# An involution's columns: how many tiles go by products of 64 channels and how many by products of 32

## The chip, the cores and the metric

The kernel runs on one core of one Trainium2 chip. The metric is the device time of one execution in microseconds, as the median of several runs.

## The reference

Four layers follow one another on an input `x` of 4 images with 256 channels of 56 x 56, in 32-bit floats. Each normalizes its input in 32 groups (`_gn`), applies a block, and adds the block's result to its input. Layers 0 and 2 are involutions, and the change is in them. An involution is a 7 x 7 filter whose taps are computed for each position and for each of 16 groups of 16 channels:

```python
t = jnp.einsum('bchw,oc->bohw', x, w1)               # 256 -> 64
t = jax.nn.relu(_bn_eval(t, ...))                    # layer 2 only
wgt = jnp.einsum('bchw,oc->bohw', t, w2) + b2[None, :, None, None]
wgt = wgt.reshape(b, G, K * K, h, w)                 # 16 groups x 49 taps
patches = jnp.stack([xp[:, :, i:i + h, j:j + w] for i in range(K) for j in range(K)], axis=2)
patches = patches.reshape(b, G, GC, K * K, h, w)
out = jnp.einsum('bgkhw,bgckhw->bgchw', wgt, patches).reshape(b, c, h, w)
out = jax.nn.relu(_bn_eval(out, ...))                # layer 2 only
```

Layer 1 is two 3 x 3 convolutions with batch norms, layer 3 a gate from channel means and Fourier transforms. They are not touched.

## The kernel before

A unit of work is one image `b` and one half `cb` of its channels (128 channels on the 128 partitions); a layer has eight units, taken one after the other. In a unit the image is cut into tiles of 3 rows by 8 columns of pixels (`TY`, `TX`): 19 tiles, one below the other, make a column, and seven columns (`NTX`) make the image. The 19th tile has two rows of image and one row of padding.

A tile with its border of 3 is a window of 9 x 14 = 126 pixels (`Q`). `begin_windows` transposes a strip of the normalized image (`strip_sb`, one column with its border) on TensorE, line L406, in seven products of 128 x 126; ScalarE copies the result into `xw` (L418), and DMAs move its rows about to make the windows of all 19 tiles (L424 and L426; in layer 0 one of the four is issued by POOL, the others by SP; in layer 2 all by SP). There are three `xw` buffers. The strip is written by POOL in layer 0 (L391) and, after the first two strips, by ScalarE in layer 2 (L389). There is one strip buffer.

Ahead of a unit's columns, `tap_matrices` builds `kt`, which holds for each group, each pixel of a tile and each tile the 126 weights that this pixel applies to the window, by products on TensorE (L593), with evictions shared by VectorE (L611) and ScalarE (L604).

`apply` then does a column. For a tile it multiplies the windows by `kt` (L635). One product takes `ng * 16` channels and the weights of `ng` groups for 24 pixels, so that for each channel one of the `ng` results is the wanted one and the others are waste: with `ng` = 4 a tile takes two products of 64 channels by 96 columns, with `ng` = 2 it takes four of 32 channels by 48. `O_PARTS` says which tiles go which way:

```python
for ng, tys, nty, rows in O_PARTS:
```

Each entry has `ng`, the first tile of each PSUM bank used, the tiles in a bank, and the rows of pixels. The wanted results are then picked out by an accumulation over `ng` terms with a scale for each channel that is one or zero (in layer 2 it holds the batch norm's scale as well): the first term by ScalarE (L648 in layer 0, L650 in layer 2), each further one by VectorE (L655), into the tile `un`. At last `un` is added to the image: by POOL in layer 0 (L660), with a relu by VectorE in layer 2 (L662).

The order in a column is: the products and evictions of both parts (`apply`), the transposes and window copies for the column three further on (`next_windows`), the next strip (`next_strip`), and then smaller work of other stages that is put between columns: statistics of the column before (L1105), in layer 0 statistics of the next image (L359), in every second unit the 1 x 1 products of the next image's bottleneck (L469), in layer 2 loads and POOL arithmetic of the gate of the image before (L803 to L816). [...] PSUM is used through four slots of two banks each, taken in turn; a column takes three: one for each part and one for the transposes.

Of the kernel before, what the change touches and what calls it, by code (L numbers as in the profile page):

```python
# [10 lines left out]
F32 = mybir.dt.float32  # L11
# [5 lines left out]
P = 128  # L17
B, C, H, W = 4, 256, 56, 56
# [15 lines left out]
TY, TX = 3, 8  # L34
# [12 lines left out]

O_PARTS = ((4, (0, 5), 5, 30), (2, (10,), 9, 26))  # L50
NXW = 3


# [18 lines left out]
def net_kernel(  # L72
# [226 lines left out]
    def involution_layer(layer, xin, xout, red, span, sb, xs_of, ahead=None, pending=None):  # L299

        with ExitStack() as es:
            wpool = es.enter_context(tc.tile_pool(name="iw", bufs=1))
            big = es.enter_context(tc.tile_pool(name="ibig", bufs=1))
            work = es.enter_context(tc.tile_pool(name="iwork", bufs=2))
            banks = es.enter_context(tc.tile_pool(name="banks", bufs=4, space=PSUM))

            def two_banks():

                return banks.tile([P, 2, 512], F32, name="ps")
# [83 lines left out]
            def window(ty):  # L393

                k, j = divmod(ty, TY)
                return (0, NSB, 2 * NSB - 1)[j] + k
# [226 lines left out]
            def apply(b, cb, kt, tx, xw):  # L623

                img = xs_of[b, cb].rearrange("p (h w) -> p h w", w=W)
                y0 = 0
                for ng, tys, nty, rows in O_PARTS:
                    pair = two_banks()
                    nb, m = len(tys), ng * GC
                    v = pair[:, :nb, : ng * nty * TP].rearrange("p i (e n) -> p i e n", e=ng)  # L630
                    for i in range(nb):
                        for k in range(nty):
                            ty = tys[i] + k
                            for j in range(P // m):
                                nc.tensor.matmul(  # L635
                                    v[m * j : m * j + m, i, :, k * TP : (k + 1) * TP],
                                    xw[:, window(ty), m * j : m * j + m],
                                    kt[:, ng * j : ng * j + ng, :, ty * NTX + tx, :],
                                    start=True,
                                    stop=True,  # L640
                                )
                    n = rows // nb * TX
                    o = [v[:, :, e, :n] for e in range(ng)]
                    un = work.tile([P, 2, O_PARTS[0][3] // 2 * TX], F32, name="un")
                    un = un.rearrange("p i n -> p (i n)")[:, : rows * TX]
                    part = un.rearrange("p (i n) -> p i n", i=nb)
                    if layer == 0:
                        nc.scalar.mul(part, o[0], bn["par"][ng][:, 0:1])  # L648
                    else:
                        nc.scalar.activation(  # L650
                            part, o[0], AF.Identity, bias=bn["t4"][:, cb : cb + 1], scale=bn["s4"][ng][:, 0, cb : cb + 1]
                        )
                    for e in range(1, ng):
                        s = bn["par"][ng][:, e : e + 1] if layer == 0 else bn["s4"][ng][:, e, cb : cb + 1]
                        nc.vector.scalar_tensor_tensor(part, o[e], s, part, ALU.mult, ALU.add)  # L655
                    dst = img[:, y0 : y0 + rows, tx * TX : (tx + 1) * TX]
                    y0 += rows
                    u = un.rearrange("p (r x) -> p r x", x=TX)
                    if layer == 0:
                        nc.gpsimd.tensor_tensor(dst, u, dst, ALU.add)  # L660
                    else:
                        nc.vector.scalar_tensor_tensor(dst, u, 0.0, dst, ALU.max, ALU.add)  # L662
# [355 lines left out]
            for u, (b, cb) in enumerate(units):  # L1018
# [24 lines left out]
                if b + 1 < B:  # L1043
                    n = 16 if layer == 0 else (26, 21)[cb]
# [57 lines left out]
                img = xs_of[b, cb].rearrange("p (h w) -> p h w", w=W)  # L1102
# [4 lines left out]
                for tx in range(NTX):  # L1107
                    if layer == 2 and u == len(units) - 1 and tx == NTX - 1:
                        column_sums(tx - 1)
                    for f in early[tx]:  # L1110
                        f()
                    apply(b, cb, kt, tx, xws[u * NTX + tx])
                    next_windows()
                    next_strip()
                    if tx > 0 and not (layer == 2 and u == len(units) - 1 and tx == NTX - 1):
                        column_sums(tx - 1)
                    for f in late[tx]:
                        f()
# [640 lines left out]
```

## Time and profile before

| What | Value |
|---|---|
| Median of three runs | 1791.4 us (1791.14 to 1792.2) |
| The profiled execution, its span | 1791.4 us |
| TensorE products busy | 1716.7 us, 96% |
| TensorE weight loads busy | 1507.5 us, 84% |
| VectorE busy | 1385.3 us, 77% |
| ScalarE busy | 813.5 us, 45% |
| POOL busy | 406.2 us, 23% |
| Products of L635, recorded | 12544, 381.8 us busy |
| Columns of layer 0 | from 72 to 515 us |
| Convolutions of layer 1 | from 515 to 1250 us |
| Columns of layer 2 | from 1285 to 1758 us |

The page gives TensorE two rows: PE for products and PEld for weight loads, which overlap. Each product of the program stands in the records as two pairs of a weight load and a product. A group's busy time is the union of its spans, so that overlapping products count once, while the mean of one is its own length, most of which lies beside its neighbours. The timeline merges neighbouring instructions of one kind into one line with their number; a note in brackets gives the engine's idle time and what ended it, and "issue" stands for time in which the engine waited for nothing that is recorded. The SP rows of the timeline are the issues of DMAs, not the transfers.

### The profile page before, as it was taken

Reading aid. Unit: us, or ns where it says so; the run is one execution under the profiler, and the core shown is the slowest. Engines: PE = TensorE matmul, PEld = TensorE weight load, DVE = VectorE, ACT = ScalarE, POOL = GpSimd, SP = SyncE. Lnnn points to the kernel's source line nnn. Section 1 sums busy time; section 2 is a strip of 40 time slices with the busy share of each in tenths; the row PEclk is TensorE's granted clock in tenths of the full one; section 3 lists DMA queues with packets and bytes.
Section 4 is the critical chain, followed back from the end, with each engine's and each line's share of the span. In section 5 each row is a group of like instructions: output and inputs, shape, how many; then the busy total and the mean of one; then the engine's idle time right before and its main releaser. Section 6 shows DMA issues by size and latency. Waiting matters only on the chain.

```text
span 1791.4 us, 55774 instructions
## 1 busy us (share of the span) xinstructions
PE 1716.7 (96%) x24040; PEld 1507.5 (84%) x24040; DVE 1385.3 (77%) x2745; ACT 813.5 (45%) x1882; POOL 406.2 (23%) x627
## 2 busy tenths in 40 slices
PE   6999999999999999999999999999999999999998
PEld 4998988889978988898889888986888887788886
DVE  2777787767778988988898889885777778687775
ACT  2555556555533222222323132111767667567564
POOL 2224422444320000000000000001000355463572
PEclk9999999999989999999999999999999999999997
DMA  2445444633653021211111111122344567566653
GB/s 86 135 151 170 140 146 134 196 107 119 204 171 105 32 75 51 76 33 64 58 68 44 52 63 37 44 110 73 122 164 156 162 213 220 169 223 189 183 154 115
DMA packets 66003, 215.76 MB, mean 120 GB/s; under 512 B 13237, under 2 KB 20926, under 8 KB 62046
## 3 DMA queue, kind: packets, MB, share of 16 engines
q1 hardware_dynamic: 49262, 145.37, 25.9%
q0 software_dynamic: 14656, 64.77, 11.3%
q8 instruction: 190, 3.11, 0.7%
q10 hardware_dynamic: 1840, 2.05, 0.4%
q14 instruction: 55, 0.45, 0.1%
HBM read 76.30 MB, written 49.15 MB: 70 GB/s over the span
## 4 chain that ended last, share of the span: by engine, by line
PE 68%; DVE 19%; ACT 4%; DMA 4%; issue 3%; POOL 2%; SPq 1%; POOLq 0%; ACTq 0%; DVEq 0%
PE mm L1523 17%; PE ps L593 14%; PE ps L635 14%; PE mm L1441 9%; DVE kt L611 6%; PE mm L1412 5%; PE ps L406 3%; DMA xw<-xw 3%; DVE un L655 3%; PE ps L469 1%; DVE res L1516 1%; DVE xs L1375 1%; DVE st L1105 1%; ACT kt L604 1%; ACT hp L488 1%
## 5 line engine op out<-in xcount | busy, mean ns | idle before, releaser
L635 PE MATMUL ps<-kt,xw 126*32 126x48 f32 (+1 forms) x12544 | 381.8, 235 | 27.8 <-issue 12.2
L635 PEld LDWEIGHTS ps<-kt,xw 126*32 126x32 f32 (+1 forms) x12544 | 341.9, 121 | 74.5 <-issue 45.5
L593 PE MATMUL ps<-hp,z_sb 64*126 64x133 f32 x6144 | 383.2, 279 | 8.4 <-DVE kt L611 4.6
L1523 PE MATMUL mm<-v,u_sb 128*128 128x280 f32 (+1 forms) x1728 | 383.5, 383 | 1.9 <-DVE u_sb L1254 1.5
L593 PEld LDWEIGHTS ps<-hp,z_sb 64*126 64x126 f32 x6144 | 363.6, 185 | 24.4 <-DVE kt L611 6.8
L611 DVE TENSOR_TENSOR kt<-ps,zb_sb 126x798 f32<-126x798 f32 x352 | 332.9, 980 | 60.4 <-PE ps L593 49.2
L1523 PEld LDWEIGHTS mm<-v,u_sb 128*128 128x128 f32 x1728 | 326.1, 189 | 56.3 <-DVE u_sb L1254 1.9
L604 ACT ACTIVATE kt<-ps,zb_sb 126x133 f32<-126x133 f32 x960 | 280.1, 441 | 107.3 <-PE ps L593 107.3
L1441 PE MATMUL mm<-v,u_sb 128*128 128x252 f32 (+1 forms) x936 | 209.5, 384 | 0.0
L1441 PEld LDWEIGHTS mm<-v,u_sb 128*128 128x128 f32 x936 | 176.4, 189 | 30.5 <-issue 0.8
L655 DVE SCALAR_TENSOR_TENSOR un<-ps,s,un 128x240 f32<-128x240 f32 x224 | 102.6, 458 | 86.7 <-ACT un L650 79.9
L1560 POOL DMA_DIRECT2D x<-xs x24 | 13.1, 547 | 680.1 <-DVE xs L1559 426.5
L655 DVE SCALAR_TENSOR_TENSOR un<-ps,par_sb,un 128x240 f32<-128x240 f32 x224 | 98.1, 457 | 86.8 <-ACT un L648 82.3
L1508 ACT ACTIVATE res<-xs,shift,norm_sb 128x1120 f32<-128x1120 f32 (+1 forms) x24 | 30.2, 1258 | 236.3 <-DVE xs L1559 107.3
L418 ACT COPY xw<-ps 126x896 f32<-126x896 f32 x112 | 101.2, 905 | 44.0 <-PE ps L406 38.5
L406 PE MATMUL ps<-ident_sb,strip_sb 128*126 128x128 f32 x784 | 111.9, 283 | 8.4 <-POOL strip_sb L391 5.3
L660 POOL TENSOR_TENSOR xs<-un,xs 128x240 f32<-128x240 f32 x112 | 72.1, 664 | 192.2 <-DVE un L655 192.1
L648 ACT ACTIVATE un<-ps,par_sb 128x240 f32<-128x240 f32 x112 | 50.1, 448 | 122.5 <-PE ps L635 120.6
L650 ACT ACTIVATE un<-ps,bn_t,s 128x240 f32<-128x240 f32 x112 | 60.1, 537 | 94.7 <-PE ps L635 88.7
L406 PEld LDWEIGHTS ps<-ident_sb,strip_sb 128*126 128x126 f32 x784 | 85.1, 142 | 19.5 <-POOL strip_sb L391 8.3
L1412 PE MATMUL mm<-xs,u_sb 128*128 128x126 f32 (+1 forms) x792 | 98.7, 277 | 2.3 <-DVE xs L1375 1.3
L1412 PEld LDWEIGHTS mm<-xs,u_sb 128*128 128x128 f32 x792 | 94.4, 191 | 3.7 <-DVE xs L1428 1.6
(256 smaller groups left out, 1903.1 us busy)
## 6 DMA issues: line engine op xcount, KB each, us to landing
xw<-xw SPq DMA_DIRECT2D x168, 252.0 KB
xw<-xw SPq DMA_DIRECT2D x224, 126.0 KB
xw<-xw POOLq DMA_DIRECT2D x56, 252.0 KB, 4.6
xs<-x SPq DMA_DIRECT2D x24, 560.0 KB
x<-xs POOLq DMA_DIRECT2D x8, 1568.0 KB, 7.5
xs<-x SPq DMA_DIRECT2D x8, 1568.0 KB
xs<-in_x_dram SPq DMA_DIRECT2D x6, 1568.0 KB
x<-xs SPq DMA_DIRECT2D x6, 1568.0 KB
```

The costliest lines, as they stand in the source:

```text
L406: nc.tensor.transpose(ps[:Q, k * P : (k + 1) * P], flat[:, k * Q : (k + 1) * Q], ident_sb)
L418: nc.scalar.copy(xw[:, :NSB, :], ps[:Q, : NSB * P].rearrange("q (n c) -> q n c", n=NSB))
L593: nc.tensor.matmul(ps[:Q, i, k * NT : (k + 1) * NT], z_sb[i * R : (i + 1) * R, cb * GB // 2 + gp, z0 : z0 + Q], hp[i * R : (i + 1) * R, py ...
L604: nc.scalar.activation(kt[:, g0 + i, pb, :, k], ps[:Q, i, k * NT : (k + 1) * NT], AF.Identity, bias=zb_sb[:, cb * GB + g0 + i, p0 + k : p0 ...
L611: nc.vector.tensor_tensor(kt[:, g0 : g0 + 2, pb], ps[:Q, :, : PB * NT].rearrange("q i (k t) -> q i t k", k=PB), zb_sb[:, cb * GB + g0 : cb ...
L635: nc.tensor.matmul(v[m * j : m * j + m, i, :, k * TP : (k + 1) * TP], xw[:, window(ty), m * j : m * j + m], kt[:, ng * j : ng * j + ng, :, ...
L650: nc.scalar.activation(part, o[0], AF.Identity, bias=bn["t4"][:, cb : cb + 1], scale=bn["s4"][ng][:, 0, cb : cb + 1])
L655: nc.vector.scalar_tensor_tensor(part, o[e], s, part, ALU.mult, ALU.add)
L660: nc.gpsimd.tensor_tensor(dst, u, dst, ALU.add)
L1412: nc.tensor.matmul(ps[:, co * m : (co + 1) * m], u[ci][:, co * P : (co + 1) * P], v2[:, e, : n // 2, ci * WT : (ci + 1) * WT], start=(ci = ...
L1441: nc.tensor.matmul(ps, u1_sb[:, ci, dy, k, co * P : (co + 1) * P], v[:, k, dy * NB + ci : (dy + n - 1) * NB + ci + 1 : NB, :], start=(j == 0),
L1523: nc.tensor.matmul(ps, u2_sb[:, ci, dy, k, co * P : (co + 1) * P], v[:, k, dy * NB + ci : (dy + n - 1) * NB + ci + 1 : NB, :], start=(j == 0),
```

## The change

Ten tiles of a column went by products of 64 channels and nine by products of 32. Now the first three go by 64 and the other sixteen by 32. A column's products in the program are 6 and 64 where they were 20 and 36. The first part fills one bank with three tiles, where it filled two with five each; the second fills two banks with eight tiles each, where it filled one with nine. It now holds 48 rows of which 47 exist, so the addition to the image is cut to the rows that exist. The tile `un` becomes two tiles of one buffer each, one for each part and of its own size, where it was one tile of two buffers.

```diff
-O_PARTS = ((4, (0, 5), 5, 30), (2, (10,), 9, 26))
+O_PARTS = ((4, (0,), 3, 9), (2, (3, 11), 8, 48))
...
-                    un = work.tile([P, 2, O_PARTS[0][3] // 2 * TX], F32, name="un")
-                    un = un.rearrange("p i n -> p (i n)")[:, : rows * TX]
+                    un = work.tile([P, rows * TX], F32, name=f"un{ng}", bufs=1)
                     part = un.rearrange("p (i n) -> p i n", i=nb)
...
-                    dst = img[:, y0 : y0 + rows, tx * TX : (tx + 1) * TX]
+                    real = min(rows, H - y0)
+                    dst = img[:, y0 : y0 + real, tx * TX : (tx + 1) * TX]
+                    u = un.rearrange("p (r x) -> p r x", x=TX)[:, :real]
                     y0 += rows
-                    u = un.rearrange("p (r x) -> p r x", x=TX)
```

The order of the instructions on each engine is as before; only the number and the shapes of those of L635 and of the evictions differ.

## The prediction

> **What bounds the kernel now.** The edit touches only the column work of the two involution layers, so I first read the 40 slices and the groups. Those layers run from 72 to 515 us and from 1285 to 1758 us, and TensorE is busy in nine tenths of nearly every slice there, at full clock. Its group of the edited line, split by shape:
>
> ```profile
> L635 PE MATMUL ps<-kt,xw 126*64 126x96 f32 x4480 | 256.6, 266 | 15.2 <-DMA xw<-xw 11.7 <-DVE un L655 2.0
> L635 PE MATMUL ps<-kt,xw 126*32 126x48 f32 x8064 | 134.5, 218 | 12.6 <-issue 12.2
> ```
>
> Each program matmul appears as two pairs of weight load and product. Means of overlapping products say little of their pace, so I went to the timeline of one undisturbed column of layer 0 (weight loads only; columns are start, length, engine, line):
>
> ```profile
> 199.37 1.99 PEld L635 LDWEIGHTS ps<-kt,xw 126*64 126x64 f32 x40 [0.17 <-issue]
> 201.53 0.99 PEld L635 LDWEIGHTS ps<-kt,xw 126*32 126x32 f32 x72 [0.16 <-issue]
> 202.60 0.74 PEld L406 LDWEIGHTS ps<-ident_sb,strip_sb 128*126 128x126 f32 x7
> 203.51 3.11 PEld L635 LDWEIGHTS ps<-kt,xw 126*64 126x64 f32 x112 [0.17 <-issue]
> ```
>
> So 40 pairs of 64 channels (ten tiles) take 201.53 - 199.37 = 2.16 us, 72 pairs of 32 channels (nine tiles) 1.07, the seven transposes 0.91: 4.14 us a column with no idle beyond the switches. A pair costs 51 ns in the first part (1.99 / 39) and 14 ns in the second (0.99 / 71). A tile is 204 ns there and 111 ns here: on paper the edit makes TensorE faster.
>
> The list of waits then has an odd line (us in total, times, longest):
>
> ```profile
> PEld ps L635 <- issue: 45.5, 152, 2.4
> ```
>
> The timeline of three columns of layer 2 shows where it comes from:
>
> ```profile
> 1299.94 0.65 PEld L635 LDWEIGHTS ps<-kt,xw 126*32 126x32 f32 x41 [0.53 <-issue]
> ...
> 1303.77 1.24 PEld L635 LDWEIGHTS ps<-kt,xw 126*32 126x32 f32 x72 [0.15 <-issue]
> ...
> 1309.64 0.45 PEld L635 LDWEIGHTS ps<-kt,xw 126*32 126x32 f32 x27 [0.88 <-issue]
> ```
>
> The 72 pairs are broken after 31, after 38 (a pause inside the 1.24) and after 45 of them, and TensorE waits there for nothing that is recorded. The break moves on by seven pairs a column. A column is 119 pairs, 238 instructions, and about four semaphore instructions, 242; 256 - 242 = 14 instructions are seven pairs. So TensorE pauses every 256 instructions. The DMA queues name the cause:
>
> ```profile
> q8 instruction: 190, 3.11, 0.7%
> ```
>
> 190 packets and 3.11 MB are 16 KB, 256 instructions of 64 bytes, a packet; 190 x 256 = 48,640 is the 48,080 instructions of TensorE plus its semaphores. These are fetches of TensorE's own program. Narrowing the DMA view, packets start at 1297.52, 1302.20, 1307.30 and 1311.50, and the three pauses end at 1299.94, 1304.47 and 1309.64: 2.3 to 2.4 us after each start. The next packet starts 1.9 to 2.8 us after a pause ended. When TensorE has run dry, a block of 256 instructions thus comes round in 2.35 + 2.3 = 4.65 us. Over the trace 25 of the 112 runs of 32 channels have such a pause over 0.25 us, 0.26 to 1.6 us, 20 us together. None of this kind is seen inside a run of 64 channels: there 128 pairs last 6.5 us.
>
> [...] in the convolution, where nothing is late, a packet starts about 300 instructions ahead of its use, one block and a little. [...]
>
> **The change part by part**, against the profiled execution of 1791.4 us (span and median of the runs are both 1791.4, so nothing has to be converted).
>
> *TensorE's work.* Removed: 28 pairs of 64 channels; added: 56 of 32. New column: 12 x 51 ns + 0.11 (the rest of 2.16 - 40 x 51) = 0.72; 128 x 14 + 0.07 = 1.85; transposes 0.91: 3.48 against 4.14. Gain 0.66 us a column if instructions are there.
>
> *TensorE's fetch.* Per column 147 pairs + 4 = 298 instructions in place of 242, 1.16 blocks. TensorE could use up a block in 3.48 / 1.16 = 3.0 us; before it took 4.14 / 0.945 = 4.4 us, just about the turn-round. So it now runs dry at nearly every block, and the turn-round F sets the pace. One unit (seven columns of one image half) has 7 x 298 - 14 = 2072 instructions, 8.1 blocks. [...] the tap products ahead of it are slow (62 ns a pair), so seven must be waited for, and what is executed ahead of the first and behind the last is about one block, 3.0 us: a unit takes 7F + 3.0. F isn't shown for a stage that is dry throughout, so I bound it: below, 3.44 us is the shortest time between two packet starts anywhere; above, pauses that follow one another in loaded columns end 5.6 and 5.1 us apart (1685.47, 1691.05, 1696.18) and once 6.0. In layer 0 they end 4.6 and 4.8 apart (328.72, 333.33, 338.09), while packets that were not late come every 4.2 us on average from 202 to 219 us. I take F = 4.4 in layer 0 (a slower column also has less DMA per us), 4.6 in the first units of layer 2 and 5.0 in those with the gate's DMA traffic.
> - Layer 0, four plain units, now 30.1, 29.3, 30.5, 29.3 us by the timeline: 33.8, so 4.0 each: 16.
> - Layer 0, three units with the next image's bottleneck products: four columns now 17.9 us on average become 3.6F + 2.9 = 18.7; two columns of 7 to 8 us with slow 504-wide products lose 0.66 and pause about 0.5; the last goes from 4.1 to 1.16F = 5.1: +1.5 each, 4.5. The last unit, half of whose columns wait for window copies: +2.
> - Layer 2: first unit 30.3 to 35.2, +4.9. Four loaded plain units, 33.2 us on average, to 38.0: +4.8 each, 19. Three with bottleneck products (34.7, 36.7, 35.8), 8.4 blocks at 4.6 to 4.8: 37.0, 38.5 and 38.5, +7.
>
> Sum +54 us.
>
> *Evictions.* The first part's shrink from 240 to 72 elements a row, the second's grow from 208 to 384. By the two rows of VectorE's L655 (468 ns for 240, 427 for 208) 72 take some 0.27 us and 384 some 0.63: a column 3 x 0.27 + 0.63 = 1.44 against 1.83. ScalarE's pair stays near 0.90 in layer 0. POOL's addition goes from 698 and 629 ns to about 0.33 and 1.0, the same sum. All this is hidden: busy time a column would be under 3.1 us on each. Only latency counts: POOL adds the second part, issues one window copy and then writes the strip that the next transposes wait for. From the end of the 32-channel run: 0.19 + ScalarE 0.58 + VectorE 0.63 + POOL 1.0 + issue 0.6 + strip 0.9 to 1.0, with gaps about 4.1 us. It meets transposes one column later, so it costs nothing at 4.9 us a column; were fetches not late it would hold layer 0 to (3.48 + 4.1) / 2 = 3.8 instead of 3.48. In layer 2 ScalarE writes the strip and this chain is absent.
>
> *Nothing.* The `un` tiles: two buffers that alternated between the two parts become one for each part, the same reuse distance. PSUM: two banks asked for as before, the first part fills 288 columns of one, the second 384 of each of two. The cut to 47 rows drops one row of padding. No DMA is added or moved. Window copies have more time: at 3.5 us a column layer 2's four issues of 0.78 us on SP would have been nearly the limit, at 5 they are not.
>
> **The rivals.**
> 1. *Faster: fetches keep up.* If F fell below about 3.9 (7F + 3.0 = 30 in layer 0; 4.3 in the loaded units), TensorE's 0.66 us would show. For it: packets 3.44 and 3.45 us apart do occur, and each column's copies spread over more time. Against: nine pauses of layer 0, at its present DMA load. Then layer 0 gains what the strip chain leaves, 2.6 us a unit, 21, and layer 2 0.66 on its 29 columns now under 4.6 us, 19: 1751 us.
> 2. *Pauses only of the size seen.* If more than one block is in flight, each block end inside a 32-channel run costs the 0.8 us of today's mean. 130 block ends, 86% of them in such runs, make 90 us; less today's 20 and the 40 of rival 1: +30, 1821 us. Against: no two packets start closer than 3.44 us.
> 3. *DMA load stretches F.* At F longer by 0.4 (a packet waits behind window copies as in 1552.44, 4.5 us after the pause before it), 107 turn-rounds (50 in layer 0, 57 in layer 2) add 43 us: 1890 us.
>
> **How the numbers follow.** The likeliest case, fetches setting the pace at 4.4 to 5.0: 52%, 1845 us, its own range 1820 to 1875. Rival 2, 20%, ends around 1800 to 1825; rival 3, 14%, above 1875; rival 1, 10%; losses and gains that cancel within 0.2% (F lower by 0.5, as 54 / 107 says), 4%. 0.2% (3.6 us) is about what a measurement of this kernel can tell from no change. Slower: 52 + 20 + 14 = 86%. The range 1797 to 1890 leaves out rival 1, most of the cancelling case and half of rival 3.
>
> **What would show it.** Right: some 214 fetch packets in place of 190; 64-channel runs of about 0.7 us and 32-channel runs with pauses of 1 us and more in nearly every column; columns of about 5 us, in layer 0 too; idle of L635's weight loads for "issue" of over 120 us; VectorE's busy time down by about 40 us and worth nothing. Wrong: columns of 3.5 to 3.8 us without pauses (rival 1), or transposes waiting for the strip in each column (the eviction chain is the bound). The weakest term is F: 0.1 us of it is 11 us of time.

## The result

| | Before | After |
|---|---|---|
| Median of four runs | 1791.8 us (1791.14 to 1798.62) | 1847.54 us (1841.98 to 1855.95) |
| Span of the profiled execution | 1791.4 us | 1841.6 us |
| TensorE's weight loads of L635 idle for "issue" | 45.5 us | 132.5 us |
| Fetch packets of TensorE's program | 190 | 214 |
| Mean granted clock of TensorE | 0.985 | 0.967 |

The ratio is 1.0305, 95% interval 1.0268 to 1.0342: the changed kernel is slower by 56 us. The page of the kernel after, from its parts on busy time, queues and groups (busy us, mean ns, then idle time ahead and what ended it):

```profile
PE 1681.6 (91%) x27176; PEld 1459.5 (79%) x27176; DVE 1355.0 (74%) x2745; ACT 808.3 (44%) x1882; POOL 408.6 (22%) x627
...
q8 instruction: 214, 3.51, 0.8%
...
L635 PEld LDWEIGHTS ps<-kt,xw 126*32 126x32 f32 (+1 forms) x15680 | 281.9, 118 | 156.7 <-issue 132.5
```

TensorE, VectorE and ScalarE all have less busy time than before (TensorE's products 1681.6 us against 1716.7), and yet the span is 50 us longer. What grew is the idle time of one group, and no engine or transfer ended it. The list of waits of the kernel after (us in total, times, longest) puts it beside the wait that the eviction chain could have caused, which stands below it for the kernel before too:

```profile
PEld ps L635 <- issue: 132.5, 182, 3.7
...
PEld ps L406 <- POOL strip_sb L391: 10.3, 13, 1.9
```

```profile
PEld ps L406 <- POOL strip_sb L391: 8.3, 9, 1.8
```

The transposes wait for POOL's strip 10.3 us in all, 8.3 before. The evictions are not it. The timeline of TensorE's weight loads in the kernel after shows a whole unit, the first of layer 2 (start, length, engine, line; in brackets the idle time ahead; a line has the shape of its first instruction, so that the 102 at 1327.30 are 12 pairs of 64 channels and 90 of 32):

```profile
1318.07 2.44 PEld L635 LDWEIGHTS ps<-kt,xw 126*64 126x64 f32 x134 [0.26 <-DVE kt L611]
1321.94 0.81 PEld L635 LDWEIGHTS ps<-kt,xw 126*32 126x32 f32 x16 [1.44 <-issue]
1322.91 1.52 PEld L635 LDWEIGHTS ps<-kt,xw 126*32 126x32 f32 x111 [0.15 <-issue]
1325.99 0.32 PEld L635 LDWEIGHTS ps<-kt,xw 126*32 126x32 f32 x17 [1.56 <-issue]
1326.38 0.75 PEld L406 LDWEIGHTS ps<-ident_sb,strip_sb 128*126 128x126 f32 x7
1327.30 2.00 PEld L635 LDWEIGHTS ps<-kt,xw 126*64 126x64 f32 x102 [0.17 <-issue]
1330.23 0.57 PEld L635 LDWEIGHTS ps<-kt,xw 126*32 126x32 f32 x38 [0.94 <-issue]
...
1334.27 0.85 PEld L635 LDWEIGHTS ps<-kt,xw 126*32 126x32 f32 x59 [0.76 <-issue]
...
1338.52 1.10 PEld L635 LDWEIGHTS ps<-kt,xw 126*32 126x32 f32 x80 [1.00 <-issue]
...
1343.04 1.38 PEld L635 LDWEIGHTS ps<-kt,xw 126*32 126x32 f32 x101 [1.23 <-issue]
...
1347.31 1.69 PEld L635 LDWEIGHTS ps<-kt,xw 126*32 126x32 f32 x122 [1.00 <-issue]
...
1352.02 0.20 PEld L406 LDWEIGHTS ps<-ident_sb,strip_sb 128*126 128x126 f32 x2 [2.42 <-issue]
```

Read the counts first. After the pause that ended at 1325.99 come 17 + 7 + 102 pairs and some semaphore instructions until the next one: 126 pairs and about four semaphores, 256 instructions. The pairs left for each column after its pause are 17, 38, 59, 80, 101, 122: 21 more each time, because a column now has 298 instructions, 42 more than a block. Once a block TensorE stands for 0.8 to 2.4 us, whatever it was in the middle of; the last pause falls among the transposes. Then read the times at which it goes on: 1321.94, 1325.99, 1330.23, 1334.27, 1338.52, 1343.04, 1347.31, 1352.02. They are 4.04 to 4.71 us apart, 4.30 on average, and seven of these steps make 30.1 of the unit's 34.8 us. This unit took 30.3 before. Narrowing the DMA view, a fetch packet starts 2.4 to 3.0 us ahead of each of these eight times.

In the whole trace, pauses over 0.25 us inside the runs of 32 channels (from the start of one weight load to the next) went from 25 (19 us) to 71 (103 us). Counted in order through the trace, with weight loads, products and semaphores, all 71 lie a multiple of 256 instructions apart, within one, and so do the 25 of before; and each of them ends 2.2 to 3.0 us after the start of a fetch packet. That marks them as pauses for the fetch. The 45.5 us of idle time before hold other things too: the longest, 2.4 us at 1740.25, is inside a run of 64 channels and off this spacing.

Over all the columns, by my sum over the records of weight loads, the time went from 531.6 to 574.4 us. Its split is an estimate, good to some 10 us, because it depends on where a pause is taken to begin: pauses for the fetch +114 us, TensorE's work -84, other waits -7, and +20 from a clock that was cut to half after long pauses, which is new. The other 7 us of the span's 50 lie outside the columns. Part of them are tap products that begin with a pause for the fetch (2.33 us at 365.4) or at the low clock (4.4 us of it behind the unit that ends at 234).

The clock shows in a table of stretches of the kernel after (start:end, length, then busy us of PE, PEld, DVE, ACT and POOL with their instructions, granted clock of TensorE, DMA share, GB/s):

```profile
199.38:219.06 19.68, 14.80 (x536) 12.61 (x526) 9.54 (x26) 6.29 (x12) 10.98 (x16) 0.91 0.57 159
204.38:207.79 3.41, 1.44 (x83) 1.22 (x73) 0.62 (x3) 0.06 (x1) 1.65 (x3) 1.00 0.69 211
207.79:211.21 3.42, 3.42 (x70) 2.86 (x72) 2.24 (x6) 1.75 (x3) 1.73 (x3) 0.50 0.15 49
211.21:214.62 3.41, 3.40 (x139) 2.85 (x130) 1.90 (x6) 1.71 (x3) 1.74 (x3) 1.00 0.77 223
```

In the second stretch TensorE is busy for 1.44 us of 3.41, because of a pause of 2.1 us. In the third its clock is 0.50, and it does 72 weight loads where it does 130 in the fourth. The half clock begins at 207.81 and lasts 3.41 us; ahead of it stand the 1.44 us of work of the second stretch. The records show when the clock is low, not what it goes by. Outside such stretches the clock is at full speed (1.00). In the stages of columns about 75 us are at half clock, in 16 stretches, against one of 3.4 us before. In the 3.41 us ahead of each of the 16, TensorE is busy for 0.1 to 1.8 us.

### The profile page after: what moved, and what is told of

Read it like the earlier page. It is cut to its first block, busy times and chain, and to the rows that moved or that the text cites. A ratio compares the mean times of both kernels' runs of the same rounds, so it can differ in the third digit from the quotient of the medians.

```text
span 1841.6 us, 62057 instructions
## 1 busy us (share of the span) xinstructions
PE 1681.6 (91%) x27176; PEld 1459.5 (79%) x27176; DVE 1355.0 (74%) x2745; ACT 808.3 (44%) x1882; POOL 408.6 (22%) x627
## 4 chain that ended last, share of the span: by engine, by line
PE 72%; DVE 13%; issue 8%; ACT 3%; DMA 2%; POOL 2%; SPq 0%; POOLq 0%; ACTq 0%; DVEq 0%
PE mm L1523 17%; PE ps L593 16%; PE ps L635 14%; PE mm L1441 10%; PE mm L1412 5%; PE ps L406 4%; DVE kt L611 4%; PE ps L469 2%; DMA xw<-xw 1%; DVE res L1516 1%; DVE xs L1375 1%; ACT kt L604 1%; DVE un L654 1%; PE ps L718 1%; POOL strip_sb L391 1%
## 5 line engine op out<-in xcount | busy, mean ns | idle before, releaser
L635 PE MATMUL ps<-kt,xw 126*32 126x48 f32 (+1 forms) x15680 | 329.1, 226 | 101.1 <-issue 98.8
L635 PEld LDWEIGHTS ps<-kt,xw 126*32 126x32 f32 (+1 forms) x15680 | 281.9, 118 | 156.7 <-issue 132.5
L654 DVE SCALAR_TENSOR_TENSOR un<-ps,par_sb,un 128x72 f32<-128x72 f32 x224 | 82.8, 371 | 120.2 <-ACT un L647 115.9
L654 DVE SCALAR_TENSOR_TENSOR un<-ps,s,un 128x72 f32<-128x72 f32 x224 | 83.5, 373 | 117.1 <-ACT un L649 113.0
L406 PE MATMUL ps<-ident_sb,strip_sb 128*126 128x128 f32 x784 | 120.8, 297 | 19.0 <-issue 8.5
L660 POOL TENSOR_TENSOR xs<-un,xs 128x72 f32<-128x72 f32 x112 | 74.1, 661 | 209.1 <-DVE un L654 194.4
L406 PEld LDWEIGHTS ps<-ident_sb,strip_sb 128*126 128x126 f32 x784 | 90.9, 149 | 31.9 <-issue 10.4
L647 ACT ACTIVATE un<-ps,par_sb 128x72 f32<-128x72 f32 x112 | 50.5, 453 | 146.7 <-PE ps L635 138.7
L649 ACT ACTIVATE un<-ps,bn_t,s 128x72 f32<-128x72 f32 x112 | 59.9, 539 | 111.3 <-PE ps L635 111.0
L149 POOL TENSOR_TENSOR norm_sb<-norm_sb,mhalf 128x1 f32<-128x1 f32 x32 | 19.7, 619 | 374.1 <-DVE norm_sb L148 374.1
```

Source lines behind the costliest of these rows:

```text
L406: nc.tensor.transpose(ps[:Q, k * P : (k + 1) * P], flat[:, k * Q : (k + 1) * Q], ident_sb)
L635: nc.tensor.matmul(v[m * j : m * j + m, i, :, k * TP : (k + 1) * TP], xw[:, window(ty), m * j : m * j + m], kt[:, ng * j : ng * j + ng, :, ...
L649: nc.scalar.activation(part, o[0], AF.Identity, bias=bn["t4"][:, cb : cb + 1], scale=bn["s4"][ng][:, 0, cb : cb + 1])
```

## Experiments

The question is whether the number of TensorE's instructions per us is the bound, or one of the other things that the edit moved (work on TensorE, evictions, `un`, PSUM), and what makes the refill of the program slow. The first four share one set of runs of the kernel before (median 1793.48), `wide` and the pair without copies another (1790.7), the last two a third (1792.67).

**Other numbers of tiles.** The same change with five tiles by 64 channels, and with one:

```diff
-O_PARTS = ((4, (0,), 3, 9), (2, (3, 11), 8, 48))
+O_PARTS = ((4, (0,), 5, 15), (2, (5, 12), 7, 42))   # n5
+O_PARTS = ((4, (0,), 1, 3), (2, (1, 10), 9, 54))    # n1
```

> Five tiles of a column by 64 channels and fourteen by 32: 282 instructions of TensorE a column, where the change has 298. Fetch sets the pace: 0.44 fewer blocks of 256 to wait for in each of 16 units, at about 4.5 us each: 31 us under the change, so about 1815 us (1805 to 1830). Only the length of TensorE's work counts: two tiles more by 64 add 0.19 us a column, 21 us: about 1868. The second part's evictions and the strip behind them are the bound: that part is 336 elements and not 384, about 0.13 us a column less: about 1833, with transposes waiting for the strip in most columns of layer 0.

> One tile of a column by 64 channels and eighteen by 32: 314 instructions a column. Fetch sets the pace: half a block more in each unit than with the change, 35 us: about 1883 us (1865 to 1900). Only TensorE's work counts: 0.19 us a column less, about 1827. Evictions and strip: 432 elements in the second part, about 0.13 us a column more: about 1862.

| Tiles by 64 channels | TensorE's products busy | Fetch packets | Median | Ratio to before |
|---|---|---|---|---|
| 10 (before) | 1716.7 | 190 | 1793.48 | |
| 5 (`n5`) | 1685.2 | 207 | 1829.64 | 1.0197 (1.016 to 1.0233) |
| 3 (after) | 1681.6 | 214 | 1847.54 | 1.0305 (1.0268 to 1.0342) |
| 1 (`n1`) | 1672.4 | 221 | 1878.49 | 1.0472 (1.0429 to 1.0515) |

The time goes with the packets and against TensorE's work. From the list of waits of `n5` and then of `n1`:

```profile
PEld ps L635 <- issue: 112.1, 163, 4.6
```

```profile
PEld ps L635 <- issue: 174.8, 217, 4.2
```

From five tiles to three and from three to one there are seven packets more each time; the median rises by 18 and by 31 us, 2.6 and 4.4 us a packet. I read this so: at the lower end some of the work taken away still shows, at the upper end each block costs about a turn-round. `n1` came within 5 us of its expectation. `n5` came 15 us above its own, at the upper end of the range, and its time alone would fit the 1833 us of the eviction rival as well. But that rival asks for transposes that wait for the strip in most columns of layer 0; in `n5` they wait 11 times, 8.4 us in all, about as in the kernel before (9 times). `n1` (1862 us by that rival) speaks against it too.

**The same number of instructions in the kernel before.** Fourteen products of one column each behind each second part, into columns of PSUM that nobody reads, give the kernel before the changed kernel's 147 pairs a column, while its evictions, `un` and PSUM stay as they are:

```diff
+                    if ng == 2:
+                        for i in range(14):
+                            j = i % 4
+                            nc.tensor.matmul(
+                                pair[m * j : m * j + m, 1, i : i + 1],
+                                xw[:, window(tys[0]), m * j : m * j + m],
+                                kt[:, 0, 0, tx, 0:1],
+                                start=True,
+                                stop=True,
+                            )
```

> The kernel before with 14 products of 32 channels by one column added to each second part, into an unused bank (results not used): 298 instructions a column as with the change, but ten tiles by 64 and the evictions of before. Fetch sets the pace: the same number of blocks as the change, about 1845 to 1865 us, with pauses for instructions in most columns. Only the work counts: 28 pairs at 14 ns are 0.4 us a column, at most 44 us, 1835, and pauses no more than in the kernel before (some 45 us of idle for no recorded cause).

It took 1873.75 us (1857.34 to 1883.04), ratio 1.0432 (1.0364 to 1.0499), with the changed kernel's 214 packets. Its waits (L645 are the added products):

```profile
PEld ps L635 <- issue: 59.0, 150, 3.8
PEld ps L645 <- issue: 22.9, 16, 4.5
```

So the kernel before becomes slow without any of the other edits, with pauses of up to 4.5 us inside the added products. It overshot the upper end of its expectation by 9 us, though. By my sum over the columns, an estimate as above, it has 84 us more than before: fetch pauses +60, work +26 (an undisturbed column grew by 0.25 us), half clock +15, other waits -17. So it does some 110 us more work than the changed kernel (+26 against -84) and ends only 26 us behind it. Why it ends behind it at all, and not level with it, was not taken apart.

**`un` alone.** The kernel before with the new allocation only:

```diff
-                    un = work.tile([P, 2, O_PARTS[0][3] // 2 * TX], F32, name="un")
-                    un = un.rearrange("p i n -> p (i n)")[:, : rows * TX]
+                    un = work.tile([P, rows * TX], F32, name=f"un{ng}", bufs=1)
```

> The kernel before with only the buffers of un changed, one for each part. Every theory of mine: no difference, 1791 us within 0.2%. If a wait of ScalarE for a buffer of un were part of the loss, it would be longer than that.

1793.04 us over 12 runs, ratio 0.9997 (0.9985 to 1.001). It is worth nothing, to within 0.15%.

**More work, the same instructions.** In the changed kernel each product of 32 channels covers 72 columns in place of 48:

```diff
+                                dst, g, gs = v[m * j : m * j + m, i, :, k * TP : (k + 1) * TP], ng * j, ng
+                                if ng == 2:
+                                    g, gs = min(g, GB - 3), 3
+                                    dst = pair[m * j : m * j + m, i, 2 * TP * k : 2 * TP * k + 3 * TP]
...
-                                    v[m * j : m * j + m, i, :, k * TP : (k + 1) * TP],
+                                    dst,
...
-                                    kt[:, ng * j : ng * j + ng, :, ty * NTX + tx, :],
+                                    kt[:, g : g + gs, :, ty * NTX + tx, :],
```

> The change with every product of 32 channels over 72 columns in place of 48 (the extra 24 are waste written over, and the wanted results are not sorted out, so the output is not the reference's). Same number of instructions; TensorE's work is half as long again in the second part, 128 pairs at 21 ns in place of 14, 0.9 us a column. Fetch sets the pace: a block's work rises from 3.0 to about 3.8 us and stays under the 4.4 to 5.0 us of a turn-round, so 1850 to 1870 us, and pauses shrink by about what the work grows. TensorE's work or the evictions behind it set the pace: 0.9 us for 112 columns come on top, about 1945.

1856.67 us (1846.47 to 1859.4), ratio to before 1.0341 (1.03 to 1.0383): inside the range expected for the fetch, and 9 us above the changed kernel, whose interval it overlaps. From its timeline of weight loads and its list of waits:

```profile
209.33 1.40 PEld L639 LDWEIGHTS ps<-kt,xw 126*32 126x32 f32 x71 [0.15 <-issue]
212.42 1.18 PEld L639 LDWEIGHTS ps<-kt,xw 126*32 126x32 f32 x57 [1.70 <-issue]
```

```profile
PEld ps L639 <- issue: 84.9, 152, 4.6
```

The 128 pairs of a column now take 1.40 + 1.18 = 2.6 us without their pause, where they took 1.8: 0.8 us more in each of 112 columns, 90 us. (TensorE's products, of which many overlap, are busy 1747.9 us in place of 1681.6.) Of this some 9 us reach the end; the wait for "issue" fell by 48, and in the stages of columns the clock is at half speed for 24 us in place of 75. Most of the time that TensorE gains or loses on these products is given to or taken from the pauses. This is the run that tells a limit by instructions from a limit by work most plainly.

**Without window copies.** If the refill takes turns with the window copies in the DMA engines, it should be faster without them. Both kernels with the loop of window copies left out, so that all products read the windows of the first row:

```diff
-                for j in range(1, TY):
-                    ...
-                    nc.sync.dma_start(xw[: Q - cut, at : at + n, :], xw[cut:Q, 0:n, :])
-                    eng = nc.sync if layer == 2 or j == 1 else nc.gpsimd
-                    eng.dma_start(xw[Q - cut : Q, at : at + n, :], xw[:cut, 1 : 1 + n, :])
...
-                                    xw[:, window(ty), m * j : m * j + m],
+                                    xw[:, window(ty) % NSB, m * j : m * j + m],
```

> The change without the DMAs that make the windows of the second and third row (products read the first row's windows in their place, so the output is not the reference's; same instructions on TensorE otherwise). If a fetch is slow because its packet waits behind window copies, the turn-round falls from about 4.6 to 3.6 us and a unit to about 28 us: about 1750 us. If the turn-round is a fixed latency, pauses stay and only waits for copies go: about 1830.

> The kernel before with the same copies left out (output not the reference's). If fetches wait behind window copies, its 25 pauses of 20 us go, and the 19 us of waits for copies: about 1755 us. If not, only the waits for copies: about 1772, with the pauses still there.

The changed kernel took 1768.18 us so, the kernel before 1761.18 (one run each). From the tables of stretches over the same 19.68 us (columns as above), first of the kernel before, then of the changed kernel without copies:

```profile
199.38:219.06 19.68, 19.68 (x589) 17.90 (x588) 12.52 (x29) 8.58 (x14) 13.17 (x20) 1.00 0.67 186
```

```profile
199.38:219.06 19.68, 17.85 (x643) 15.93 (x645) 13.67 (x32) 8.60 (x19) 11.31 (x15) 1.00 0.07 24
```

The share of the DMA engines falls from 0.57 in the kernel after to 0.07, and in the same time 645 weight loads are done in place of 526, with no stretch at half clock. (The comparison flatters the run without copies: this stretch of the kernel after lies in the slowest plain unit of layer 0, 39.4 us long.) Yet the pauses have not gone. From the timeline and the waits of the changed kernel without copies:

```profile
200.73 0.86 PEld L628 LDWEIGHTS ps<-kt,xw 126*32 126x32 f32 x60 [0.45 <-issue]
...
204.74 1.09 PEld L628 LDWEIGHTS ps<-kt,xw 126*32 126x32 f32 x80 [0.75 <-issue]
```

```profile
PEld ps L628 <- issue: 88.7, 168, 2.5
```

There are still 71 pauses in the 32-channel runs, now of 71 us. The block ends are 4.01 us apart at 200.73 and 204.74; over neighbouring blocks of the whole trace that both end in such a pause, the mean is 3.98 us, 3.74 in layer 0 and 4.24 in layer 2, against 4.64, 4.83 and 4.48 with the copies. In the kernel before the 25 pauses become one. So the copies lengthen the turn-round by about 0.7 us (without the three blocks that touch half clock the 4.64 is 4.62), and even without them a block takes longer than the 3.0 us in which TensorE could use it up. Hence the miss, between the two expectations: leaving out the copies, with all waits for them, is worth 79 us to the changed kernel and 30 to the kernel before. The difference of the two kernels shrinks from 56 to 7 us; with one run each, and 14 us between the lowest and the highest run of the changed kernel, these 7 are not told from nothing. That the edit does not show a gain of its own lies above all in the pauses that are left: the waits of the kernel before without copies have 25.8 us for "issue" in place of 88.7, 63 us less, against the edit's gain of 0.66 x 112 = 74 us in work. That would leave a gain of 11 us where a loss of 7 was measured; these 18 us were not taken apart.

```profile
PEld ps L628 <- issue: 25.8, 123, 1.6
```

**No small products.** All 19 tiles by 64 channels, in three parts, with `un` named by the rows:

```diff
-O_PARTS = ((4, (0,), 3, 9), (2, (3, 11), 8, 48))
+O_PARTS = ((4, (0, 5), 5, 30), (4, (10,), 5, 15), (4, (15,), 4, 12))
```

> All nineteen tiles of a column by 64 channels, in three parts of ten, five and four tiles: 83 pairs and some four semaphore instructions, 170 instructions a column in place of 242. Fetch: a block lasts a column and a half, about 7 us, longer than any turn-round seen, so no pause inside the products, and the 19 us of them in the kernel before go. TensorE's work: nine tiles at 204 ns and not 111 add 0.8 us a column where TensorE sets the pace, and VectorE's picking out, three further terms for every tile, comes to about 5 us a column. So slower than before for the opposite reason, about 1855 us (1840 to 1890), without pauses.

1889.16 us, ratio to before 1.0549 (1.0535 to 1.0562): within its range, but at the very top, 34 us above the figure expected. The page and the list of waits:

```profile
PE 1801.3 (95%) x20008; PEld 1596.9 (85%) x20008; DVE 1557.1 (83%) x3361; ACT 848.6 (45%) x1994; POOL 419.5 (22%) x683
...
q8 instruction: 158, 2.59, 0.6%
```

```profile
PEld ps L635 <- issue: 34.5, 99, 1.1
```

No pause for the fetch is left in these products (99 waits of 0.35 us on average, the longest 1.1 us, and none of those inside a run lies on the spacing of 256), and now the work counts: 4.8 to 4.9 us a column in layer 0, and in layer 2 up to 6.7 us, with VectorE at 1557 us for its added terms. In the chain that ended last VectorE has 30%, where it had 19% before, so part of the loss is VectorE's and not TensorE's; the two were not separated. Of the numbers tried ten tiles are the best: below, the fetch costs more than the smaller products save, and with 19 the work of the two engines does.

**A version that beats both.** In the kernel before, the transposes behind the second column of units of layer 0 wait for POOL's strip, and POOL issues one of four window copies ahead of that strip. With all of them on SP:

```diff
-                    eng = nc.sync if layer == 2 or j == 1 else nc.gpsimd
+                    eng = nc.sync
```

> The kernel before with all four window copies of a column issued by SP in layer 0, where POOL issued one. If POOL's copies with their packets of 6 KB are what holds up fetches in layer 0, its nine pauses (6 us) go; the strip is ready 0.6 us sooner, which shortens the wait behind the second column of its eight units by about 5 us: about 1781 us. If SP's fourth issue of 0.8 us makes windows late instead: 1795 us or more.

1787.63 us over 15 runs against 1792.67 over 20 of the kernel before: ratio 0.9969 (0.9955 to 0.9983). That is a small gain, half of the 10 us expected. The timeline of weight loads, first of the kernel before, then of this one:

```profile
198.46 0.75 PEld L406 LDWEIGHTS ps<-ident_sb,strip_sb 128*126 128x126 f32 x7 [0.93 <-POOL strip_sb L391]
```

```profile
196.19 0.99 PEld L635 LDWEIGHTS ps<-kt,xw 126*32 126x32 f32 x72 [0.15 <-issue]
197.26 0.75 PEld L406 LDWEIGHTS ps<-ident_sb,strip_sb 128*126 128x126 f32 x7
```

The wait of 0.93 us is gone (what follows the 32-channel run at once, 0.08 us behind it, are the transposes), and in the whole trace the transposes' waits for the strip fell from 8.3 to 4.2 us. The pauses for the fetch inside the 32-channel runs fell as well, from 25 to 9 (19 to 10 us). But the idle time for "issue" as a whole did not:

```profile
PEld ps L635 <- issue: 47.5, 151, 3.4
```

It was 45.5 us before. Pauses off the spacing of 256 grew in its place, inside runs of 64 channels, the longest of them 3.4 us. And the trace of `un_only`, which is no faster than the kernel before, has 19 pauses (14 us) where that has 25, so that some of the fall can be chance. The strip's 4 us are the more likely source of the 5 us gained; no run shows it.

## Why the prediction was right, and where its sum was off

- **Fetch sets the pace**, the likeliest case: shown. 1845 us forecast, 1847.5 measured. The packets (214), the 64-channel runs (0.74 to 0.77 us where undisturbed, 0.72 forecast), the 32-channel runs (1.79 to 1.84 against 1.85), the gain of 0.66 us (the undisturbed first column of a unit went from 3.63 to 2.97), the columns (median 5.0 us in layer 0 and 4.7 in layer 2, "about 5" forecast) and the idle time for "issue" are as forecast. Pauses of 1 us and more in nearly every column are not: 71 of the 112 columns have a pause inside the 32-channel run, and 47 have one of 1 us or more. Of the rivals, the one in which fetches keep up falls with 71 pauses, the one with pauses of 0.8 us with their mean of 1.4 us, and the third, a longer turn-round throughout, with its 1890 us.
- **Layer 0.** The means are as forecast, and partly by luck. Plain units went from 29.8 to 33.7 us (33.8 forecast), but three of the four took 31.3, 32.2 and 31.7 us, and the one from 194.8 us took 39.4, with 12 us of pauses where the three have 4 to 7, and 9 us at half clock. In the first of the three, packets start 3.4 us apart at 80.99, 84.42 and 87.82 us and TensorE, which has waits of 0.4 to 0.6 us for the strip there, goes through without a pause for them: here the fetch kept up, as the first rival says. Units with bottleneck products took 1.65 us more each (1.5 forecast), as the mean of -0.8, +4.9 and +0.9; the last 2.2 (2 forecast).
- **A unit is 7F + 3.0.** Seven turn-rounds, an estimate of mine that no trace of before showed, are right in the unit shown above. The constant is not: there the first block ended 4.3 us after the unit began and 0.4 us remained behind the last, 4.7 in place of 3.0. The 3.0 counted work at full pace, and that work has a pause of its own.
- **F.** It was taken as 4.4 us in layer 0, 4.6 in layer 2 and 5.0 in its loaded units. Neighbouring blocks that both end in a pause are 4.83 us apart in layer 0 and 4.48 in layer 2, with a range of 3.5 to 6.6: F is no fixed number, and the later units did not have the larger one. With the larger constant the plain loaded units went to 36.9 us, by 3.7 each where 4.8 was forecast, 15 us for four in place of 19.
- **Layer 2's units with bottleneck products**, +2.3 each forecast: this step failed. They took 32.5, 38.0 and 37.1 us, 35.9 on average, and 35.7 before. The sum (7.4 turn-rounds and the 3.0 for 8.4 blocks) charged every block behind the first with a full turn-round. But the bottleneck products are slow work with few instructions (196 recorded products of L469, 586 ns each at the median), and behind them the fetch is ahead again: in the unit from 1380.2 to 1412.7 the seven columns have four pauses over 0.25 us in their 32-channel runs, 2.4 us in all, and it went from 34.7 to 32.5 us: the 0.66 us a column is a gain there.
- **What made up for it.** The sum over the columns was +54 (its parts make 53.4), and +43 was measured. Seven us came from outside the columns, which the sum left out, and the median lies 4 us above the profiled execution (1843.4). That 1845 came so near the measured time is thus partly luck. The clock at half speed was not foreseen at all. Its 20 us are inside the +43, but how much of them reaches the end is open: `wide` shows that most of the time that products lose comes off the pauses. The direction and the mechanism do not rest on it.
- **Evictions are hidden**: right. VectorE's busy time fell by 30 us rather than 40. The picking out took 38 us less (a term of 72 elements takes 0.29 us, one of 384 takes 0.62), and the additions of layer 2 rose by 2. It is worth nothing, as the strip's wait of 10 us and `tiny` show. `un`: nothing, as `un_only` shows. The other use of PSUM was not tested by itself; TensorE's waits for ScalarE's first terms, which free it, come to some 3 us in the columns.

Still open: some turn-rounds last 6 us and more (1462.02, 1468.61, 1474.75), with a packet that starts up to 3.8 us after the pause before it. These are columns with the gate's transfers, but no run separates them, and the 6.2 us from 200.45 to 206.65 lie in layer 0, which has none. Nor was the half clock tested apart from the pauses that go before it.

## What to carry over

Count an engine's instructions per us as well as its work. Here 256 instructions of TensorE take some 4.6 us to come when it waits for them beside window copies and 4.0 without, so by my estimate a stage of this kernel that would run above about 55 to 64 instructions per us (256 by 4.6 and by 4.0) is bound by them, and smaller, quicker products can make it slower. Look for "issue" pauses that move on by the same number of pairs each round and sit a fixed number of instructions apart; then trade columns of work against instructions (`wide` got 66 us more of TensorE's busy time for 9 us). Slow work with few instructions between the dense runs, as the bottleneck products are here, and DMAs moved away from them are two more things to try; no run here tried them as remedies.

## What the hardware showed that was not expected

- Pauses of about 2 us and more were often followed by 3.41 us, or multiples of it up to 13.65, at half of TensorE's clock, in a stage that is otherwise busy (16 of the 25 pauses over 1.9 us in the stages of columns); seven transposes then take 1.6 to 1.7 us in place of 0.91. By my estimate they add 20 us to the work in the columns, beside 114 us more of pauses.
- The window copies slow the refill of this kernel's program: 4.64 us a block with them (share of the DMA engines 0.57 in the stretch above), 3.98 without (0.07).
